# A graph convolution on one core: one-hot rows made for two quads at once, a node number read as float32 out of two bfloat16 columns, and unit additions placed ahead of the equality

## The chip, the cores and the metric

The kernel runs on one core of a Trainium2 chip. The metric is the device time of one execution in microseconds. A core has five engines with queues of their own: TensorE (PE; its weight loads are shown as PEld), VectorE (DVE), ScalarE (ACT), GpSimd (POOL) and SyncE (SP), which here only issues transfers. Engines wait for each other through semaphores.

## The reference

There are 6,250 nodes with 128 features and 200,000 edges. The layer normalises the nodes, multiplies them by `W_in`, fetches a row for each edge, multiplies it by a filter worked out from 20 edge attributes, sums the products at the edges' other ends, and applies two more small layers and a residual:

```python
h = jnp.maximum(_layernorm(x, axis=-1), 0.0)
x = atomic_embedding @ W_in                      # atomic_embedding is h
W_ij = shifted_softplus(f_ij @ W_f1 + b_f1) @ W_f2 + b_f2
W_ij = W_ij * f_ij_cutoff
x_ij = x[idx_j] * W_ij                           # idx_j = dst, sorted
out = jax.ops.segment_sum(x_ij, idx_i, num_segments=N_ATOMS)   # idx_i = src, in random order
return shifted_softplus(out @ W_o1 + b_o1) @ W_o2 + b_o2       # added to x
```

`dst` is sorted, so the rows fetched by neighbouring edges lie close together. `src` is random, so the sum at the end touches all nodes at any time.

## The kernel before, in words

**Quads.** Edges are taken in chunks of 128 and in quads of four chunks (512 edges), 391 quads in all. Two quads make a super-chunk, which SP loads four quads ahead (`load_sc`): edge attributes `ft`, source numbers `sb`, relative row numbers `rb` (one transfer for each quad, into the lower or the upper 64 partitions) and `wn`, windows of 21 consecutive node rows, each in three bfloat16 parts.

**One iteration of the main loop** (from L938) works on several quads at once, in an order written out by hand: every engine gets its instructions in the order of the program text. For quad q: PE makes `z` (L287); ACT makes `e` in three steps (L292, L293, L298); DVE makes the one-hot rows `oh` (L306) that say which window row each edge takes, and `a` (L321); PE multiplies `oh` by `wn` into `xg` (L336) and `a` by `w2` into `W` (L344); ACT scales `xg` into `xc` (L349); DVE multiplies both into messages (L354).

**The plain quads.** 247 quads end in a scatter. DVE compares source numbers into `eq` (L315), PE multiplies `eq` by the messages into `pp` (L366), so that edges of one chunk with the same source share a sum, and ACT copies this into `s` (L374; five buffers). DVE works out `jf` (L388) and ACT the row numbers `ji` (L395). POOL then issues an indirect transfer for each chunk, which adds rows of `s` to one of four accumulators in DRAM (L414), four to a quad. Two scatters into the same accumulator run one after the other.

**The sorted quads.** The other 144 quads, about three in eight, avoid the scatter. Their edges are given one of 16 groups of 392 nodes (`rank_group` and what follows), with 32 slots for each group. DVE makes the permutation `pm` (L499) from `iot`, a row of counting numbers; the messages in `pt` are split in place into three bfloat16 parts (L513), and `ext` puts two more columns behind them (L516): the node's number in its group less 196, and the group. PE permutes all that into `pq` (L523), ACT casts it to `mst` (L531), and DVE adds 196 to the number again to make `lo` (L535). Six sorted quads together make a round, which is summed in four units: DVE makes one-hot columns `so` from `iot` and `lo` (L604), PE multiplies (72 matmuls, L619) into four PSUM buffers, all that the tag B has, and DVE adds these to `accT` in SBUF (L628, L630). What does not fit in the slots is the overflow: two sorted quads share a buffer `mo`, go through an equality of their own (`over_idx`, `over_dg`, `over_row`, `over_eq`, `over_sum`) and end in one scatter.

**Hooks.** Everything beside the plain path is hung on points of an iteration with `at(i, point, ...)`: "D0", "D1", "DM" and "D2" stand between DVE's instructions, "A0" to "A2" between ACT's, "PE2" after PE's, "L" ahead of the iteration, "S" after the scatters. So a hook says in which iteration and behind which instruction its work is queued. On the same hooks, from quad 7 on and every nine quads, hang the 24 further groups of nodes that are normalised and multiplied by `W_in` (`prep_*`), and the splitting of the edge attributes (`fb_*`).

**The tail** (from L1058) loads three of the accumulators, adds them to `accT` and applies the two last layers.

The functions that the change touches:

Of the kernel before, what the change touches and what calls it, by code (L numbers as in the profile page):

```python
# [32 lines left out]
PW = 386  # L33
# [11 lines left out]
def tile_gnn(ctx: ExitStack, tc: tile.TileContext, x, fB, cT, srcT, srcr, dstr, win_, wf1, wf2, bias, bo1c, wo1,  # L45
# [19 lines left out]
    ACC_R = NP + P  # L65
    ZR = 10 if ACC_R % 10 == 0 else 1
# [3 lines left out]
    GN = NP // GRP  # L70
# [50 lines left out]
    iot = cp.tile([P, SLOTS], F16, name="iot")  # L121
# [179 lines left out]
    def s1_oh(q):  # L301
        rb = loads[q // 2][2]
        j = q % 2
        oh = wk.tile([P, 512], BF16, tag="oh", name="oh")
        v = slice(j * HB, (j + 1) * HB)
        nc.vector.tensor_scalar(oh[v], rb[v], rowid[v], None, op0=ALU.is_equal)  # L306
        st[q]["oh"] = oh
# [116 lines left out]
    def rank_group(r):  # L424
        qs = mpq[RKQ * r:RKQ * r + RKQ]
        nc4 = 4 * len(qs)
        srcf = wk.tile([P, 4 * RKQ], F32, tag="srcf", name="srcf", bufs=1)
        for k, q, d, n in runs(qs):
            o = srcf[:, 4 * k:4 * (k + n)]
            nc.vector.tensor_copy(o if n == 1 else o.rearrange("p (j c) -> p j c", c=4), quad_cols(srcT_sb, q, d, n))  # L430
        srcf = srcf[:, :nc4]
        n = [P, nc4, GRP - 1]
        nc.vector.tensor_tensor(ge[:, :nc4, 1:GRP], srcf.unsqueeze(2).to_broadcast(n),
                                thr.unsqueeze(1).to_broadcast(n), op=ALU.is_ge)
        G = wk.tile([P, 4 * RKQ, GRP], BF16, tag="G", name="G", bufs=1)
# [91 lines left out]
    def perm_out(q, s):  # L527
        a, b = divmod(s, 2)
        if b == 0:
            mp[q]["ms", a] = wk.tile([P, 2, PW], BF16, tag=f"ms{a}", name="mst", bufs=RND + 2 + 2 * a)  # L530
        nc.scalar.copy(mp[q]["ms", a][:, b], mp[q].pop(("q", s))[:, :PW])  # L531

    def perm_loc(q, a):
        lo = wk.tile([P, 2], F32, tag=f"lo{a}", name="lo", bufs=RND + 2 + 2 * a)
        nc.vector.tensor_scalar(lo, mp[q]["ms", a][:, :, 3 * P], float(GN // 2), None, op0=ALU.add)  # L535
        mp[q]["lo", a] = lo

    def over_pe(q):
        h = mpi[q] % 2 * OVC
        t = ps.tile([P, 512], F32, tag="B", name="po", bufs=4)  # L540
        o = t[h:h + OVC]
        for c in range(4):
            w = mp[q]["pm"][:, c, GRP * CAP:]
            pt = high(mp[q]["pt"][:, c:c + 1])[:, 0]
            nc.tensor.matmul(o[:, :P + 2], w, pt[:, 2 * P:PW], start=(c == 0), stop=False)
            nc.tensor.matmul(o[:, :P], w, pt[:, P:2 * P], start=False, stop=False)
            nc.tensor.matmul(o[:, :P], w, pt[:, :P], start=False, stop=(c == 3))
        mp[q]["po"] = t

    def over_out(q):  # L550
        h = mpi[q] % 2 * OVC
        mo = mos[mpi[q] // 2 % 2]
        nc.scalar.copy(mo[h:h + OVC, :P + 2], mp[q].pop("po")[h:h + OVC, :P + 2])

    def over_idx(q):
        mo = mos[mpi[q] // 2 % 2]
        so = sp_.tile([P, 1], F32, tag="ovs", name="ovs", bufs=2)
        nc.vector.scalar_tensor_tensor(so, mo[:, P + 1:P + 2], float(GN), mo[:, P:P + 1], op0=ALU.mult, op1=ALU.add)
        mp[q]["so"] = so

    def over_dg(q):
# [3 lines left out]
        jd = sp_.tile([P, 2], F32, tag="ojd", name="ojd", bufs=2)  # L565
# [13 lines left out]
    def over_sum(q):  # L579
        t = ps.tile([P, 512], F32, tag="B", name="osum", bufs=4)  # L580
        nc.tensor.matmul(t[:, :P + 3], mp[q]["eq"], mos[mpi[q] // 2 % 2][:, :P + 3], start=True, stop=True)
        mp[q]["sum"] = t

    def over_copy(q):
        s = sp_.tile([P, 132], F32, tag="os", name="os", bufs=2)
        nc.scalar.copy(s[:, :P + 3], mp[q].pop("sum")[:, :P + 3])
        mp[q]["os"] = s

    def over_ji(q):
        s, jd = mp[q]["os"], mp[q]["jd"]  # L590
        nc.vector.scalar_tensor_tensor(jd[:, 1:2], s[:, P + 2:P + 3], wgt2, jd[:, 0:1], op0=ALU.is_lt, op1=ALU.mult)
# [71 lines left out]
    with tc.manual_schedule():  # L663
# [9 lines left out]
        nc.gpsimd.iota(iot, pattern=[[1, SLOTS]], base=0, channel_multiplier=0, allow_small_or_imprecise_dtypes=True)  # L673
# [86 lines left out]
        for mo_ in mos:  # L760
            nc.vector.tensor_copy(mo_[:, P + 2:P + 3], wgt)
# [142 lines left out]
        for q in mpq:  # L904
# [33 lines left out]
        for i in range(max(NQ + 7, last + 14, r0_end + 2)):  # L938
# [358 lines left out]
```

## Time and profile before

| what | value |
|---|---|
| median of 3 runs | 2198.53 us (2196.79 to 2199.58) |
| the profiled execution: time, span | 2198.7 us, 2196.8 us |
| mean granted TensorE clock | 0.962 |
| PE, weight loads | 1913.6 us (87%), 1373.2 us (63%) |
| DVE | 1886.5 us (86%), 5123 instructions |
| ACT | 1787.2 us (81%) |
| POOL | 1751.8 us (80%) |
| scatters issued by POOL (L414) | 987 of 1621 ns and 72 of 1613 ns |

The span runs from the first to the last instruction; what lies around it is 1.9 us. A group's line in the profile gives: line, engine and operation, what it writes and reads, how often, then its busy time in us and the mean of one in ns, then the idle time of its engine just before it and what ended that. "issue" is time in which an engine waited for nothing that the profile shows. A row of the timeline gives start and duration in us, and in brackets the idle time before. A line of the waits gives the total in us, the number of times and the longest.

### The profile page before, as it was taken

How to read it: one execution, taken by the hardware profiler on the slowest of the kernel's cores; microseconds unless marked ns; L12 is line 12 of the kernel's file. 1: busy time of each engine (PE TensorE's matmuls, PEld its weight loads, DVE VectorE, ACT ScalarE, POOL GpSimd, SP SyncE). 2: the span in 40 equal slices, each digit the busy share in tenths (PEclk: the TensorE clock that was granted, in tenths of full speed). 3: DMA queues.
4: the chain of work that ended last, by engine and by line, in shares of the span. 5: the costliest groups of instructions: out<-in, count | busy, mean ns of one | idle time of the engine just before them, and what ended most of it. 6: DMA issues, size and time to landing. Idle time of an engine off the chain costs nothing.

```text
span 2196.8 us, 55656 instructions
## 1 busy us (share of the span) xinstructions
PE 1913.6 (87%) x19201; PEld 1373.2 (63%) x19201; DVE 1886.5 (86%) x5123; ACT 1787.2 (81%) x4749; POOL 1751.8 (80%) x1101
## 2 busy tenths in 40 slices
PE   3779899898989989988988999999999989899946
PEld 2556666666656666666666667666666666666724
DVE  5688999988888988898989999989889889898935
ACT  4688888888879887878888989888889888888814
POOL 2678888888888887878778888888888888888884
PEclk9799999999999999999999999999999999999977
DMA  8977777776767676767677667677767766767638
GB/s 263 248 168 145 132 143 144 141 143 125 148 128 145 132 145 129 144 122 148 131 138 143 134 136 148 124 142 144 143 121 148 136 140 129 142 127 152 129 37 235
DMA packets 396414, 316.96 MB, mean 144 GB/s; under 512 B 91839, under 2 KB 335722, under 8 KB 396130
## 3 DMA queue, kind: packets, MB, share of 16 engines
q1 hardware_dynamic: 242546, 240.57, 37.2%
q0 software_dynamic: 153296, 72.75, 33.9%
q8 instruction: 151, 2.47, 0.5%
q14 instruction: 133, 1.09, 0.2%
q10 hardware_dynamic: 288, 0.07, 0.0%
HBM read 173.32 MB, written 139.90 MB: 143 GB/s over the span
## 4 chain that ended last, share of the span: by engine, by line
DVE 34%; PE 20%; ACT 18%; DMA 10%; POOL 9%; issue 7%; SPq 2%; ACTq 0%; DVEq 0%; POOLq 0%
POOL acc L414 9%; DMA acc<-s,ji 6%; PE pq L523 4%; ACT xc L349 4%; PE W L344 4%; PE pp L366 4%; DVE pt L513 4%; DVE so L604 3%; DVE pm L499 3%; DVE a L321 3%; DVE eq L315 3%; ACT mst L531 3%; DVE accT L630 3%; PE un L619 3%; ACT e L293 2%
## 5 line engine op out<-in xcount | busy, mean ns | idle before, releaser
L414 POOL DMA_INDIRECT acc<-s,ji x987 | 1599.8, 1621 | 375.7 <-issue 237.3
L523 PE MATMUL pq<-pt,pm 128*128 128x386 bf16 x2304 | 461.6, 340 | 32.8 <-ACT s L374 26.1
L344 PE MATMUL W<-w,a 128*128 128x128 f32 x3128 | 467.0, 294 | 0.0
L349 ACT ACTIVATE xc<-xg,cT_sb 128x128 f32<-128x128 f32 x1564 | 447.1, 374 | 18.0 <-PE xg L336 14.4
L344 PEld LDWEIGHTS W<-w,a 128*128 128x128 f32 x3128 | 391.3, 196 | 42.5 <-issue 3.3
L619 PE MATMUL un<-so,mst 32*128 32x392 bf16 x6912 | 337.6, 330 | 40.7 <-DVE pr L463 9.4
L366 PE MATMUL pp<-m,eq 128*128 128x129 f32 x1976 | 282.9, 287 | 83.2 <-DVE accT L630 61.2
L523 PEld LDWEIGHTS <-pm 128*128 128x128 bf16 x2304 | 225.6, 99 | 190.1 <-issue 46.2
L366 PEld LDWEIGHTS pp<-m,eq 128*128 128x128 f32 x1976 | 263.6, 197 | 125.3 <-DVE accT L630 86.9
L619 PEld LDWEIGHTS <-mst 32*128 32x128 bf16 x6912 | 208.8, 94 | 164.2 <-issue 60.2
L321 DVE SCALAR_TENSOR_TENSOR a<-z,e 128x512 f32<-128x512 f32 x391 | 266.4, 681 | 49.3 <-ACT e L298 47.3
L374 ACT COPY s<-pp 128x258 f32<-128x258 f32 x494 | 175.1, 393 | 147.2 <-PE pp L366 90.7
L298 ACT ACTIVATE e<-e,con 128x512 f32<-128x512 f32 x391 | 282.4, 722 | 12.7
L293 ACT ACTIVATE e<-e 128x512 f32<-128x512 f32 x391 | 246.5, 631 | 12.4
L531 ACT CAST mst<-pq 128x386 bf16<-128x386 f32 x576 | 246.6, 479 | 10.2 <-PE pq L523 10.2
L292 ACT ACTIVATE e<-z 128x512 f32<-128x512 f32 x391 | 238.6, 610 | 16.2 <-PE z L287 15.9
L630 DVE TENSOR_TENSOR accT<-un,accT 128x392 f32<-128x392 f32 x368 | 182.0, 554 | 38.9 <-PE un L619 23.2
L513 DVE TENSOR_TENSOR pt<-pt 128x512 f32<-128x512 f32 x288 | 198.3, 689 | 0.0
L354 DVE TENSOR_TENSOR m<-W,xc 128x512 f32<-128x512 f32 x247 | 168.1, 681 | 33.7 <-ACT xc L349 28.2
L499 DVE TENSOR_SCALAR pm<-iot,pos 128x576 bf16<-128x576 f16 x576 | 190.4, 392 | 0.0
L354 DVE TENSOR_TENSOR pt<-W,xc 128x512 f32<-128x512 f32 x144 | 99.1, 688 | 87.8 <-ACT xc L349 77.3
L315 DVE TENSOR_TENSOR eq<-sb,srcT_sb 128x512 f32<-128x512 int16 x247 | 168.3, 682 | 3.1
(156 smaller groups left out, 2768.4 us busy)
## 6 DMA issues: line engine op xcount, KB each, us to landing
sb<-src SPq DMA_DIRECT2D x195, 256.0 KB
ft<-fsd SPq DMA_DIRECT2D x195, 240.0 KB
rb<-reld SPq DMA_DIRECT2D x391, 64.0 KB
fsd<-f SPq DMA_DIRECT2D x49, 480.0 KB
acc<-s,ji POOLq DMA_INDIRECT x987
fb<-in_fB_dram SPq DMA_DIRECT2D x49, 320.0 KB
fsd<-f SPq DMA_DIRECT2D x49, 320.0 KB
wn<-tab SPq DMA_DIRECT2D x782, 15.8 KB
```

The lines of the kernel that those rows point to most:

```text
L293: nc.scalar.activation(e, e, AF.Exp, scale=-1.0)
L298: nc.scalar.activation(e, e, AF.Ln, bias=half, scale=0.5)
L321: nc.vector.scalar_tensor_tensor(a, st[q]["z"], 0.0, st[q]["l"], op0=ALU.max, op1=ALU.add)
L344: nc.tensor.matmul(W[:, c, :], st[q]["a"][:, c * P:(c + 1) * P], w2, start=False, stop=(c == 3))
L349: nc.scalar.mul(xc[:, c, :], st[q]["xg"][:, c, :], cT_sb[:, 4 * q + c:4 * q + c + 1])
L354: nc.vector.tensor_tensor(m[:, :, :P], st[q]["W"], st[q]["xc"], op=ALU.mult)
L366: nc.tensor.matmul(pp[:, c, :129], st[q]["eq"][:, k, :], m[:, k, :129], start=True, stop=True)
L414: nc.gpsimd.indirect_dma_start(out=accs[k][:, :], out_offset=bass.IndirectOffsetOnAxis(ap=ji, axis=0), in_=s, in_offset=None, compute_op=A ...
L513: nc.vector.tensor_tensor(pt[:, :, k * P:(k + 1) * P], a, high(a), op=ALU.subtract)
L523: nc.tensor.matmul(t[:, :PW], mp[q]["pm"][:, c, s * P:(s + 1) * P], high(mp[q]["pt"][:, c:c + 1, :PW])[:, 0], start=(c == 0), stop=(c == 3))
L531: nc.scalar.copy(mp[q]["ms", a][:, b], mp[q].pop(("q", s))[:, :PW])
L619: nc.tensor.matmul(ts[g][:, :GN], mp[q]["ms", s // 2][v, s % 2, k * P:(k + 1) * P], mp[q]["oh"][v], start=(q == qs[0] and k == 0), stop=(q ...
```

## The change

- `s1_oh` is carried out for even quads only and makes the one-hot rows of both quads of a super-chunk in one instruction on 128 partitions.
- `ext` gets a third column, zero, ahead of the number. A float32 whose lower half is zero and whose upper half is a bfloat16 has the bfloat16's value, so `unit_oh` reads the pair of columns of `mst` as one float32 scalar. The counting row gets 196 more numbers in front (-196 to -1), so that no addition is needed; `perm_loc` and its two hooks go. Rows of `pt` have 387 words for 386, rows of `mst` 388 for 386, and the overflow's columns move by one.
- `over_dg` hangs on "A0" of the next iteration, where it was on "A2", with three buffers for `ovs` and `ojd` where there were two.
- In the main loop the hooks of "D1" (the unit additions) stand ahead of `s1_eq`.

```diff
-PW = 386
+PW = 387
+MW = 388
...
-    iot = cp.tile([P, SLOTS], F16, name="iot")
+    iotw = cp.tile([P, GN // 2 + SLOTS], F16, name="iot")
+    iot = iotw[:, GN // 2:]
...
     def s1_oh(q):
-        rb = loads[q // 2][2]
-        j = q % 2
-        oh = wk.tile([P, 512], BF16, tag="oh", name="oh")
-        v = slice(j * HB, (j + 1) * HB)
-        nc.vector.tensor_scalar(oh[v], rb[v], rowid[v], None, op0=ALU.is_equal)
-        st[q]["oh"] = oh
+        if q % 2 == 0:
+            rb = loads[q // 2][2]
+            oh = wk.tile([P, 512], BF16, tag="oh", name="oh")
+            v = slice(0, min(2, NQ - q) * HB)
+            nc.vector.tensor_scalar(oh[v], rb[v], rowid[v], None, op0=ALU.is_equal)
+            late["oh"] = oh
+        st[q]["oh"] = late["oh"]
...
-        ext = wk.tile([P, 4 * RKQ, 2], BF16, tag="ext", name="ext")
-        nc.vector.tensor_scalar(ext[:, :nc4, 0], loc[:, :nc4], float(-GN // 2), None, op0=ALU.add)
-        nc.vector.tensor_copy(ext[:, :nc4, 1], cnt[:, :nc4])
+        ext = wk.tile([P, 4 * RKQ, 3], BF16, tag="ext", name="ext")
+        nc.vector.memset(ext[:, :, 0], 0.0)
+        nc.vector.tensor_scalar(ext[:, :nc4, 1], loc[:, :nc4], float(-(GN // 2)), None, op0=ALU.add)
+        nc.vector.tensor_copy(ext[:, :nc4, 2], cnt[:, :nc4])
...
-            mp[q]["ms", a] = wk.tile([P, 2, PW], BF16, tag=f"ms{a}", name="mst", bufs=RND + 2 + 2 * a)
-        nc.scalar.copy(mp[q]["ms", a][:, b], mp[q].pop(("q", s))[:, :PW])
-
-    def perm_loc(q, a):
-        lo = wk.tile([P, 2], F32, tag=f"lo{a}", name="lo", bufs=RND + 2 + 2 * a)
-        nc.vector.tensor_scalar(lo, mp[q]["ms", a][:, :, 3 * P], float(GN // 2), None, op0=ALU.add)
-        mp[q]["lo", a] = lo
+            mp[q]["ms", a] = wk.tile([P, 2, MW], BF16, tag=f"ms{a}", name="mst", bufs=RND + 2 + 2 * a)
+        nc.scalar.copy(mp[q]["ms", a][:, b, :PW], mp[q].pop(("q", s))[:, :PW])
...
             so = wk.tile([P, GN], BF16, tag="so", name="so", bufs=RND)
-            nc.vector.tensor_scalar(so, iot[:, :GN], mp[q]["lo", s // 2][:, s % 2:s % 2 + 1], None, op0=ALU.is_equal)
+            w = mp[q]["ms", s // 2].bitcast(F32)
+            nc.vector.tensor_scalar(so, iotw[:, :GN], w[:, s % 2, 3 * P // 2:3 * P // 2 + 1], None, op0=ALU.is_equal)
...
-        nc.gpsimd.iota(iot, pattern=[[1, SLOTS]], base=0, channel_multiplier=0, allow_small_or_imprecise_dtypes=True)
+        nc.gpsimd.iota(iotw, pattern=[[1, GN // 2 + SLOTS]], base=-(GN // 2), channel_multiplier=0, allow_small_or_imprecise_dtypes=True)
...
-            at(q + 4, "DM", perm_loc, q, 0)
-            at(q + 5, "DM", perm_loc, q, 1)
             at(q + 4, "PE2", over_pe, q)
             at(q + 5, "A0", over_out, q)
             if mpi[q] % 2:
                 at(q + 5, "DM", over_idx, q)
-                at(q + 5, "A2", over_dg, q)
+                at(q + 6, "A0", over_dg, q)
...
             if i < NQ:
                 s1_oh(i)
+            run(i, "D1")
             if 0 <= i - 1 < NQ:
                 s1_eq(i - 1)
-            run(i, "D1")
```

More of the change, by code (lines that the diff above doesn't have):

```diff
@@ L65, in tile_gnn @@
     ACC_R = NP + P
+    GN = NP // GRP
     ZR = 10 if ACC_R % 10 == 0 else 1
@@ L69, in tile_gnn @@
     CE = min(128, EP // P)
-    GN = NP // GRP
     mpq = sorted_quads(NQ)
@@ L544, in over_pe @@
             pt = high(mp[q]["pt"][:, c:c + 1])[:, 0]
-            nc.tensor.matmul(o[:, :P + 2], w, pt[:, 2 * P:PW], start=(c == 0), stop=False)
+            nc.tensor.matmul(o[:, :P + 3], w, pt[:, 2 * P:PW], start=(c == 0), stop=False)
             nc.tensor.matmul(o[:, :P], w, pt[:, P:2 * P], start=False, stop=False)
@@ L552, in over_out @@
         mo = mos[mpi[q] // 2 % 2]
-        nc.scalar.copy(mo[h:h + OVC, :P + 2], mp[q].pop("po")[h:h + OVC, :P + 2])
+        nc.scalar.copy(mo[h:h + OVC, :P + 3], mp[q].pop("po")[h:h + OVC, :P + 3])
     def over_idx(q):
         mo = mos[mpi[q] // 2 % 2]
-        so = sp_.tile([P, 1], F32, tag="ovs", name="ovs", bufs=2)
-        nc.vector.scalar_tensor_tensor(so, mo[:, P + 1:P + 2], float(GN), mo[:, P:P + 1], op0=ALU.mult, op1=ALU.add)
+        so = sp_.tile([P, 1], F32, tag="ovs", name="ovs", bufs=3)
+        nc.vector.scalar_tensor_tensor(so, mo[:, P + 2:P + 3], float(GN), mo[:, P + 1:P + 2], op0=ALU.mult, op1=ALU.add)
         mp[q]["so"] = so
@@ L564, in over_dg @@
         mp[q]["dg"] = dg
-        jd = sp_.tile([P, 2], F32, tag="ojd", name="ojd", bufs=2)
+        jd = sp_.tile([P, 2], F32, tag="ojd", name="ojd", bufs=3)
         nc.scalar.activation(jd[:, 0:1], mp[q]["so"], AF.Identity, bias=off)
@@ L580, in over_sum @@
         t = ps.tile([P, 512], F32, tag="B", name="osum", bufs=4)
-        nc.tensor.matmul(t[:, :P + 3], mp[q]["eq"], mos[mpi[q] // 2 % 2][:, :P + 3], start=True, stop=True)
+        nc.tensor.matmul(t[:, :P + 4], mp[q]["eq"], mos[mpi[q] // 2 % 2][:, :P + 4], start=True, stop=True)
         mp[q]["sum"] = t
@@ L585, in over_copy @@
         s = sp_.tile([P, 132], F32, tag="os", name="os", bufs=2)
-        nc.scalar.copy(s[:, :P + 3], mp[q].pop("sum")[:, :P + 3])
+        nc.scalar.copy(s[:, :P + 4], mp[q].pop("sum")[:, :P + 4])
         mp[q]["os"] = s
@@ L590, in over_ji @@
         s, jd = mp[q]["os"], mp[q]["jd"]
-        nc.vector.scalar_tensor_tensor(jd[:, 1:2], s[:, P + 2:P + 3], wgt2, jd[:, 0:1], op0=ALU.is_lt, op1=ALU.mult)
+        nc.vector.scalar_tensor_tensor(jd[:, 1:2], s[:, P + 3:P + 4], wgt2, jd[:, 0:1], op0=ALU.is_lt, op1=ALU.mult)
     def over_int(q):
@@ L760, in tile_gnn @@
         for mo_ in mos:
-            nc.vector.tensor_copy(mo_[:, P + 2:P + 3], wgt)
+            nc.vector.tensor_copy(mo_[:, P + 3:P + 4], wgt)
         if NQ > 2:
```

## The prediction

> **What bounds the kernel now.** I read the page's engine totals first, then the groups of instructions, then GpSimd's timeline and its waits stage by stage. The totals alone mislead:
>
> ```profile
> PE 1913.6 (87%) x19201; PEld 1373.2 (63%) x19201; DVE 1886.5 (86%) x5123; ACT 1787.2 (81%) x4749; POOL 1751.8 (80%) x1101
> DVE 34%; PE 20%; ACT 18%; DMA 10%; POOL 9%; issue 7%; SPq 2%; ACTq 0%; DVEq 0%; POOLq 0%
> ```
>
> Four engines lie between 80 and 87%, and the chain that ended last (second line) gives VectorE (DVE) the most. By these, less work on DVE would be worth much. But the costliest group of all is the scatter that GpSimd (POOL) issues, with a mean of 1.62 us and idle time before it that nothing but "issue" ends:
>
> ```profile
> L414 POOL DMA_INDIRECT acc<-s,ji x987 | 1599.8, 1621 | 375.7 <-issue 237.3 <-ACT ji L395 49.3 <-DMA acc<-s,ji 35.4
> ```
>
> In POOL's timeline (start, duration, idle before) one scatter follows the other with the same 0.30 us between them; only now and then a longer gap, ended by ScalarE's (ACT's) index `ji`, shows that POOL had run dry:
>
> ```profile
> 1601.58 1.54 POOL L414 DMA_INDIRECT acc<-s,ji  x1 [0.30 <-issue]
> 1603.43 1.54 POOL L414 DMA_INDIRECT acc<-s,ji  x1 [0.31 <-ACT mst L531]
> 1605.28 1.54 POOL L414 DMA_INDIRECT acc<-s,ji  x1 [0.30 <-issue]
> ...
> 973.14 1.54 POOL L414 DMA_INDIRECT acc<-s,ji  x1 [0.30 <-issue]
> 978.98 1.60 POOL L414 DMA_INDIRECT acc<-s,ji  x1 [4.29 <-ACT ji L395]
> ```
>
> The 0.30 us is a fixed price of each scatter, not a wait. So POOL's own account is: first scatter at 48.87 us; 1059 scatters of 1.620 = 1716.0; 1058 fixed gaps of 0.305 = 322.7; longer gaps beyond the fixed one 52.6; last scatter ends at 2140.1; the tail to 2196.8 takes 56.7. POOL is full from 49 to 2140 us but for those 52.6 us. Stage by stage they are: up to 350 us 30.6, 350 to 860 us 0.1, 860 to 1215 us 19.5, 1215 to 2020 us 0.1, after that 2.5. The early ones, and the last 2.5, mostly name the landing of an earlier scatter (one to three of the four buffers are in use early, so a scatter waits for an earlier one into the same buffer); there the index had been ready for about 20 us. Only the stage from 860 to 1215 us is short of indices. Waits of POOL in that stage (total, times, longest), and ACT's waits in it and, after the dots, from 1500 to 2020 us:
>
> ```profile
> POOL acc L414 <- issue: 41.2, 135, 0.3
> POOL acc L414 <- ACT ji L395: 23.1, 12, 6.1
> ACT s L374 <- PE pp L366: 22.3, 18, 3.1
> ...
> ACT s L374 <- DMA acc<-s,ji: 21.4, 11, 3.7
> ```
>
> The twelve waits hold 23.1 us, of which 12 fixed gaps are 3.7: 19.5 us are real. Later the pressure is reversed: ACT waits for a buffer `s` (five of them) that POOL has not emptied. I measured the lead as the time from the end of `ji` to the quad's first scatter: about 20 us from 100 to 450 us (the five buffers), falling to 4 by 700 us, 0 to 5 from 760 to 1215 us, and back at 20 by 1500 us, where it stays to the end. The quads are slower than POOL while the 24 node groups are prepared beside them (to about 1170 us), and faster afterwards.
>
> **The change, part by part.** The groups concerned:
>
> ```profile
> L306 DVE TENSOR_SCALAR oh<-rb,con 64x512 bf16<-64x512 bf16 x391 | 141.8, 363 | 8.7 <-DMA rb<-reld 2.4
> L535 DVE TENSOR_SCALAR lo<-mst 128x2 f32<-128x2 bf16 x288 | 72.9, 253 | 15.4 <-ACT mst L531 13.1
> L315 DVE TENSOR_TENSOR eq<-sb,srcT_sb 128x512 f32<-128x512 int16 x247 | 168.3, 682 | 3.1
> L366 PE MATMUL pp<-m,eq 128*128 128x129 f32 x1976 | 282.9, 287 | 83.2 <-DVE accT L630 61.2 <-ACT s L374 10.9 <-DVE accT L628 4.8
> L563 ACT ACTIVATE dg<-idt,ovs 128x128 f32<-128x128 f32 x72 | 29.3, 407 | 52.2 <-DVE ovs L558 52.0
> L513 DVE TENSOR_TENSOR pt<-pt 128x512 f32<-128x512 f32 x288 | 198.3, 689 | 0.0
> ```
>
> *One-hot rows for two quads.* 391 instructions of 64x512 become 196 of 128x512. Duration goes with the columns, so 195 x 0.363 = 70.8 us leave DVE. The pair needs both `rb` transfers of its super-chunk, the second issued some 0.5 us after the first; all were loaded four quads ahead, and the `wn` rows that the same matmuls need are issued after both, so the wait costs nothing (without that lead, at most 0.6 us a pair). Each tile now serves four quads' time instead of two, more room than before.
>
> *The node read as float32.* 288 `lo` leave: 72.9 us, and the 13.1 us that DVE waits there for `mst`. Against it: 18 memsets of 128x32 (nearest: the 128x32 cast into `ext`, 0.234), 4.2 us; four more elements in each of the 144 copies into `pt` (0.189 each), under 1 us. `so` keeps its shape and count, only its scalar comes from `mst`, ready long before. Permutes get one column: 2304 x 0.340/386 = 2 us of PE; with the overflow's extra columns under 1 us more; the evacuations 576 x 0.479/386 = 0.7 us of ACT. The longer iota (0.61 us for 576 columns, 0.82 for 772) adds 0.2 us to POOL at 7 us, hidden by the index load that lands at 13 us.
>
> *Sum for DVE:* 70.8 + 72.9 - 5 = 139 us of 1886, 7%.
>
> *Unit additions ahead of the equality.* 46 of the 96 units have an `eq` that now follows the four additions. It stood 0.60 us ahead of them (start to start), and TensorE (PE), whose four B banks the unit holds, waits 61.2 us for `accT`: up to 46 x 0.6 = 28 us less. Moved behind, `eq` delays `a` of the next quad by nothing, since both were already behind the additions; it is late only where the additions wait for the last unit matmul (23.2 us in all, 11 times), and it is read one iteration later.
>
> *`dg` one iteration later.* ACT no longer waits 52 us for `ovs`. Its two instructions (0.407 + 0.287) now stand ahead of the `mst` casts, `ji` and `xc` of the next iteration; they stood in this queue before. `orow` on PE needs `dg` in the same iteration: around 1010 us ACT's point A0 runs some 2 us ahead of PE's point, so I cost it at 0; if that lead is gone, `orow` and the permutes behind it wait up to the 0.69 us, 72 times, 50 us. SP's queue and the order of the scatters are as before.
>
> *What this does to the end.* On the chain from 350 to 1215 us, `oh` has 21.5 us (half goes: 10.7), `lo` 6.9, and `eq` ahead of additions about 41/96 of 28 = 12: 30 us, without the waits of ACT. The quads lost 19 us of lead and 19.5 of gaps there, 38.5 in all. Relief of 19.5 is enough to close the gaps; 30 leaves 11 us of lead. So the 19.5 us go, and nothing more: the other 110 us saved on DVE become idle time under a full POOL. What is late next is the scatter itself.
>
> *Does a scatter get shorter?* Its median is 1.543 and its mean 1.620, in all 82 us over the median. I sorted the scatters by what DVE ran beside them: 143 with none of the suspects 1.556, 37 with an `oh` alone 1.561, 46 with `lo` alone 1.544, 42 with `pm` alone 1.605, 7 with `eq` alone 1.819. [...] By the trace, `oh` and `lo` cost nothing and `eq`, which stays, costs 0.26. I follow the trace: 1 us, and keep 21 for the low end.
>
> *What speaks against.* `pt` gets rows of 387 words, so rows 1 and 3 begin on an odd word. No row of the trace has that. [...]
>
> *Total:* 2198.7 (profiled execution: span 2196.8 and 1.9 around it) - 19.5 - 1 = 2178.2. The profiled time lies 0.2 us over the median 2198.53, so nothing is corrected. A measurement of this kernel can tell about 0.2%, 4.4 us, from no change.
>
> **The rivals.**
> 1. *DVE is a bound throughout.* Then 139 us times its 34% of the chain, plus PE's 28: about 75 us, 2124. Against it: 0.1 us of gaps in 1315 us of two stages. Chance 0.03.
> 2. [...] Chance 0.08.
> 3. *The relief misses the stage:* `oh` and `lo` go, but the chain moves to PE and ACT, half of the gaps stays: 2188. Chance 0.14.
> 4. *Scatters lengthen.* DVE's two-input work now piles up in bursts beside them. Stage means were 1.604 to 1.637; at 1.637 throughout, 1059 x 0.017 = 18 us come back: 2196, no change. Chance 0.08.
> 5. *Odd rows slow PE.* A permute matmul reads rows of `pt`; if the 1152 that read an odd row took twice the 0.17 us that they are apart, PE would get 196 us more. 83 us of it fall before 1215 us, less 30 of relief: 53 us of new gaps, 2198.7 + 53 = 2252. It decides from a loss of 30 us in that stage, 0.06 us a matmul. For it: PE is 90% busy there. Against it: the reads already step over every second half-word at full rate. Chance 0.05.
>
> The main case has 0.62.
>
> **How the numbers follow.** The main case spans 2170 to 2184 (gaps 0 to 5 us left, stage means of the scatter moving by 0.008 either way). With rival 3 and part of 2, 2163 to 2191 leaves out rival 1, rivals 4 and 5 and some of 2: 0.2. Faster: main 0.62, rivals 1 to 3 0.25, less 0.02: 0.85. Same: most of rival 4 and a little of 3: 0.09. Slower: rival 5 and the far end of 4: 0.06.
>
> **What would show it.** Right: POOL's waits for `ji` from 860 to 1215 us fall from 23.1 to under 5 us; scatters still of 1.62 us with 0.30 between them; the lead stays over 5 us at 1000 us; ACT's waits for the landing of `acc` grow; DVE busy near 1747. `oh` x196 at about 0.36. Wrong: gaps of over 0.4 us still adding to 20 us after 350 us; a scatter mean under 1.60 or over 1.635; `pt` over 0.70 or `pq` slower by 10%. A span under 2160 would refute POOL as the bound.

## The result and the profile after

| | before | after |
|---|---|---|
| median, 4 runs of each on one chip | 2197.66 us (2194.13 to 2199.58) | 2160.73 us (2158.51 to 2169.22) |
| ratio after / before, 95% interval | | 0.9841 (0.9811 to 0.9871) |
| profiled execution: time, span, mean granted clock | 2198.7, 2196.8 us, 0.962 | 2169.22, 2166.6 us, 0.960 |

The changed kernel is 37 us faster; 2178 was forecast, with a range that ended at 2163. The profiled execution of the changed kernel is the slowest of its four, 8.5 us over their median. A second profile of it, taken with the first experiment, has a span of 2156.5 us and stands nearer to the median, so both are used below.

First the page's engine totals of the changed kernel, and under them its chain of waits by engine:

```profile
PE 1910.9 (88%) x19201; PEld 1371.3 (63%) x19201; DVE 1769.9 (82%) x4658; ACT 1781.2 (82%) x4749; POOL 1733.1 (80%) x1101
ACT 23%; PE 20%; DVE 16%; POOL 15%; DMA 15%; issue 9%; SPq 2%; ACTq 0%; DVEq 0%; POOLq 0%
```

DVE's busy time falls by 116.6 us and its part of the chain by more than half. The shares still name no bound. The groups (busy time and mean of one, then the idle time before and its releaser) answer to those shown of before:

```profile
L417 POOL DMA_INDIRECT acc<-s,ji x987 | 1583.2, 1604 | 360.3 <-issue 235.1 <-DMA acc<-s,ji 49.0 <-ACT ji L398 27.4
L308 DVE TENSOR_SCALAR oh<-rb,con 128x512 bf16<-128x512 bf16 x195 | 72.5, 372 | 2.6 <-DMA rb<-reld 2.6
L318 DVE TENSOR_TENSOR eq<-sb,srcT_sb 128x512 f32<-128x512 int16 x247 | 168.3, 681 | 0.0
L369 PE MATMUL pp<-m,eq 128*128 128x129 f32 x1976 | 273.7, 282 | 39.1 <-DVE accT L630 22.6 <-ACT s L377 6.1 <-ACT mst L535 3.9
L562 ACT ACTIVATE dg<-idt,ovs 128x128 f32<-128x128 f32 x72 | 28.2, 392 | 2.9 <-DVE ovs L557 2.9
L517 DVE TENSOR_TENSOR pt<-pt 128x512 f32<-128x512 f32 x288 | 198.7, 690 | 0.0
L527 PE MATMUL pq<-pt,pm 128*128 128x387 bf16 x2304 | 464.6, 341 | 52.5 <-ACT s L377 47.2 <-ACT h L198 2.7 <-DVE pt L517 1.7
```

The first line is the surprise: the mean scatter went from 1621 to 1604 ns, although nothing about a scatter was changed. Next POOL's waits from 860 to 1215 us, the three largest (total, times, longest), and ACT's largest wait for a landing in the whole span:

```profile
POOL acc L417 <- issue: 45.6, 149, 0.5
POOL acc L417 <- ACT mst L535: 2.7, 9, 0.3
POOL acc L417 <- DMA acc<-s,ji: 2.7, 9, 0.3
...
ACT s L377 <- DMA acc<-s,ji: 71.2, 39, 6.0
```

No wait of that stage is longer than 0.5 us: the index is always there, and it is ACT that now waits for POOL to empty `s`. POOL's account, with all 1059 scatters in it, each 0.305 us behind the last (322.7 us in every column):

| us | before | after | after, second profile |
|---|---|---|---|
| first scatter starts | 48.9 | 49.3 | 49.2 |
| 1059 scatters, total (mean) | 1716.0 (1.620) | 1696.9 (1.602) | 1692.5 (1.598) |
| gaps beyond 0.305, total | 52.6 | 39.7 | 34.9 |
| of these from 860 to 1215 us | 19.5 | 0.2 | 0.0 |
| last scatter to end of span | 56.7 | 58.0 | 57.2 |

The spans of the first two columns differ by 30.2 us: 19.1 from shorter scatters, 12.9 from gaps, less 1.7 in start and tail. The gaps lost 19.3 in the stage that was short of indices and got 6.4 back elsewhere, all at waits for landings. So the gaps of that stage went as forecast, 19.3 of 19.5 us; the shorter scatters were not forecast.

### The profile page after: what moved, and what is told of

Same layout as the page of the kernel before. It is cut to its first block, busy times and chain, and to the rows that moved or that the text cites. A ratio compares the mean times of both kernels' runs of the same rounds, so it can differ in the third digit from the quotient of the medians.

```text
span 2166.6 us, 55320 instructions
## 1 busy us (share of the span) xinstructions
PE 1910.9 (88%) x19201; PEld 1371.3 (63%) x19201; DVE 1769.9 (82%) x4658; ACT 1781.2 (82%) x4749; POOL 1733.1 (80%) x1101
## 4 chain that ended last, share of the span: by engine, by line
ACT 23%; PE 20%; DVE 16%; POOL 15%; DMA 15%; issue 9%; SPq 2%; ACTq 0%; DVEq 0%; POOLq 0%
POOL acc L417 15%; DMA acc<-s,ji 12%; ACT xc L352 5%; PE un L619 5%; PE W L347 5%; ACT e L295 3%; ACT mst L535 3%; PE pq L527 3%; ACT e L294 3%; PE pp L369 3%; ACT e L300 3%; ACT s L377 2%; DVE pm L503 2%; DVE so L604 2%; DVE a L324 1%
## 5 line engine op out<-in xcount | busy, mean ns | idle before, releaser
L417 POOL DMA_INDIRECT acc<-s,ji x987 | 1583.2, 1604 | 360.3 <-issue 235.1
L527 PE MATMUL pq<-pt,pm 128*128 128x387 bf16 x2304 | 464.6, 341 | 52.5 <-ACT s L377 47.2
L352 ACT ACTIVATE xc<-xg,cT_sb 128x128 f32<-128x128 f32 x1564 | 445.8, 373 | 25.1 <-PE xg L339 22.6
L619 PE MATMUL un<-so,mst 32*128 32x392 bf16 x6912 | 342.8, 333 | 40.3 <-DVE rm L217 11.1
L619 PEld LDWEIGHTS <-mst 32*128 32x128 bf16 x6912 | 201.4, 95 | 177.9 <-issue 62.0
L369 PE MATMUL pp<-m,eq 128*128 128x129 f32 x1976 | 273.7, 282 | 39.1 <-DVE accT L630 22.6
L295 ACT ACTIVATE e<-e 128x512 f32<-128x512 f32 x391 | 246.5, 630 | 12.4
L535 ACT CAST mst<-pq 128x387 bf16<-128x387 f32 x576 | 246.9, 481 | 11.6 <-PE pq L527 11.6
L289 PE MATMUL z<-ft,ws 123*128 123x512 bf16 x391 | 152.9, 392 | 19.5 <-DMA ft<-fsd 10.3
```

The source lines that it names most:

```text
L295: nc.scalar.activation(e, e, AF.Exp, scale=-1.0)
L352: nc.scalar.mul(xc[:, c, :], st[q]["xg"][:, c, :], cT_sb[:, 4 * q + c:4 * q + c + 1])
L369: nc.tensor.matmul(pp[:, c, :129], st[q]["eq"][:, k, :], m[:, k, :129], start=True, stop=True)
L417: nc.gpsimd.indirect_dma_start(out=accs[k][:, :], out_offset=bass.IndirectOffsetOnAxis(ap=ji, axis=0), in_=s, in_offset=None, compute_op=A ...
L527: nc.tensor.matmul(t[:, :PW], mp[q]["pm"][:, c, s * P:(s + 1) * P], high(mp[q]["pt"][:, c:c + 1, :PW])[:, 0], start=(c == 0), stop=(c == 3))
L535: nc.scalar.copy(mp[q]["ms", a][:, b, :PW], mp[q].pop(("q", s))[:, :PW])
```

## The experiments

Two theories stood after that. *Theory A, the lock:* a `tensor_scalar` on VectorE holds scatters up for as long as it runs, as the 1.605 us of the 42 scatters beside `pm` alone may say (1.556 beside none of the suspects); so taking away 288 `lo` and 195 `oh` shortens scatters. That was my assumption. *Theory B, the beginning:* something about how the equality comes to stand beside the start of a scatter. Each experiment was run beside the kernel before on the same chip; ratios are to that.

**The changed kernel again,** for a second profile and as the base of what follows.

> The changed kernel once more, as the base of the runs beside it. Its first profile closed the gaps of GpSimd between 860 and 1215 us (19.5 to 0.2 us, as forecast) and had scatters of 1.602 us where the kernel before had 1.620, which was not forecast; its median was 2160.7 us, its profiled run 2169.2. If the shorter scatter belongs to the change, the mean is again near 1.60 and the time 2157 to 2166 us. If it was the spread between executions, the mean comes out anywhere from 1.60 to 1.62 and the time up to 2178 us.

Measured: 2159.81 us against 2198.53, ratio 0.983 (0.9816 to 0.9845).

**One part taken back at a time.** From the changed kernel: the one-hot rows made for each quad again, as the removed lines of the diff have it; `lo` made again (288 instructions, read by `so`); the equality ahead of the additions again, with `over_dg` on "A2" of its old iteration.

```diff
# lo made again
+        nc.vector.tensor_scalar(lo, mp[q]["ms", a][:, :, 3 * P + 1], float(GN // 2), None, op0=ALU.add)
...
# equality first again
-                at(q + 6, "A0", over_dg, q)
+                at(q + 5, "A2", over_dg, q)
...
-            run(i, "D1")
             if 0 <= i - 1 < NQ:
                 s1_eq(i - 1)
+            run(i, "D1")
```

> The changed kernel with one-hot rows made for each quad again (391 instructions of 64x512). [...] Rival (these instructions cost a scatter nothing, as the sorting in the prediction had it; the gain was lead alone): under 3 us, since the lead of 5 to 10 us at 1100 us shrinks but does not run out.

> The changed kernel with the 288 small additions that make the node number back in their old places, and the one-hot columns reading their result. [...] Rival: under 3 us, as GpSimd stays full.

> The changed kernel with the equality ahead of the unit additions again and the overflow's diagonal back one iteration earlier on ScalarE. No work is added on VectorE, so the lock theory gives scatters of the same length and, as the lead covers the later additions, 0 to 3 us. Rival (the order is what shortened the scatters, by parting the one-hot instruction from the two-input equality behind it): the scatter mean rises by 0.005 to 0.015, the time by 5 to 15 us.

| taken back | median us | ratio (interval) | scatters, total | gaps 860 to 1215 |
|---|---|---|---|---|
| nothing | 2159.8 | 0.983 (0.9816 to 0.9845) | 1692.5 | 0.0 |
| the merged one-hot | 2177.0 | 0.9898 (0.988 to 0.9916) | 1705.0 | 6.1 |
| no `lo` | 2167.7 | 0.986 (0.9844 to 0.9876) | 1696.6 | 0.0 |
| the order, `dg` | 2166.5 | 0.9857 (0.9839 to 0.9874) | 1694.7 | 9.3 |

The one-hot rows are the part that shortens scatters (12.5 us, where two profiles of the changed kernel differ by 4.4). The order acts through gaps alone: the mean scatter rose by 0.002 us, as the first reading of that run had it, but not with its 0 to 3 us. Its line of POOL's waits from 860 to 1215 us is the old one in small:

```profile
POOL acc L417 <- ACT ji L398: 12.3, 10, 5.0
```

`lo` cost 8 us, where the rival had under 3. Its trace has 4.1 us more of scatters and 4.0 more of gaps than the second profile of the changed kernel, but the first profile has as much of both; so where the 8 us lie is not shown.

**The one-hot rows alone.** The kernel before with only the new `s1_oh`.

> The kernel before with one-hot rows for two quads at once and nothing else of the change. Lock theory and lead together: scatters shorter by 0.012 us (12 us), and of the 19.5 us of gaps some 7 to 10 gone: 2176 to 2181 us. Rival (the part works only together with the others): over 2185 us.

Measured: 2168.37 us against 2198.93, ratio 0.9867 (0.9846 to 0.9889). The scatters come to 1689.1 us, as short as in the whole change, while 11.8 us of gaps stay in the middle stage. This part alone brings 31 of the 39 us, and is 8 us faster than the range expected of it. Its group of scatters:

```profile
L415 POOL DMA_INDIRECT acc<-s,ji x987 | 1575.5, 1596 | 369.5 <-issue 234.8 <-DMA acc<-s,ji 48.9 <-ACT ji L396 45.0
```

**The lock, tested by putting work back.** To the changed kernel, one more DVE instruction for every odd quad, so that it stands where the second `oh` was: a memset (no `tensor_scalar`, so without a lock by Theory A), a one-hot of 128 rows whose result is not used, or an equality of 192 columns that isn't used either.

```diff
         st[q]["oh"] = late["oh"]
+        if q % 2:                                    # memset
+            pad = wk.tile([P, 272], F32, tag="pad", name="pad")
+            nc.vector.memset(pad, 0.0)
...
+            # or: 128 rows, one input
+            nc.vector.tensor_scalar(pad, loads[q // 2][2], rowid, None, op0=ALU.is_equal)
...
+            # or: two inputs, 192 columns
+            nc.vector.tensor_tensor(pad, loads[q // 2][1][:, :192].rearrange("p (c i) -> p c i", c=2),
+                                    srcT_sb[:, q * 4:q * 4 + 2].unsqueeze(2).to_broadcast([P, 2, 96]), op=ALU.is_equal)
```

> The changed kernel with one instruction more on VectorE in each odd quad, where the second one-hot instruction stood: a memset of 128x272 float32 into a tile that nobody reads, about 0.35 us, 68 us in all. [...]Lock theory: the scatter mean stays at 1.598 to 1.602; only the lead shrinks, and the gaps from 860 to 1215 us come back by about 7 us as in the kernel with split one-hot rows; the time is 2162 to 2170 us. Rival (any work on VectorE at this place lengthens scatters, by moving the two-input instructions behind it): the mean rises to 1.610 and the time to about 2177 us.

> The same with a one-hot instruction (tensor_scalar, 128x512 bfloat16 from SBUF to SBUF, about 0.35 us) into a tile that nobody reads. Lock theory: as with split one-hot rows, a scatter mean of about 1.610 and 2174 to 2180 us, so 8 to 12 us more than with the memset of the same length at the same place. Rival: the same as with the memset.

> The same with a small equality of two SBUF inputs (tensor_tensor, 128x192, about 0.36 us) into a tile that nobody reads. In the sorting of the kernel before, scatters beside the large equality were the longest (1.82 us). [...]

By source line in each kernel's trace (shortest/mean/longest in ns, then where in the span) the one-hot and the two-input pad cost DVE the same, the memset a little less:

```profile
L313 DVE MEMSET pad<- x195: 285/285/285, 28.0 to 2051.4; 128x272 f32 x195
L313 DVE TENSOR_SCALAR pad<-rb,con x195: 334/349/634, 28.1 to 2052.8; 128x512 bf16<-128x512 bf16 x195
L313 DVE TENSOR_TENSOR pad<-sb,srcT_sb x195: 337/351/391, 27.9 to 2054.1; 128x192 f32<-128x192 int16 x195
```

All three are by ratio about 9 us slower than the changed kernel: 2169.21, 2170.12 and 2170.40 us, ratios 0.9868, 0.987 and 0.987. The scatters' means were 1.605, 1.596 and 1.603, the gaps of the middle stage 0.3, 8.5 and 3.8 us. Theory A expected the longest scatters beside the one-hot, at 1.610; they are shortest there. Of the memset it expected 1.598 to 1.602 and some 7 us of gaps; that was missed too. An extra 68 us of one-hots leaves the scatters at 1690.2 us in all, 2.3 under the second profile, so their lengthening does not follow the busy time of such instructions; what this run lost is gaps.

The lock itself is there all the same, when single scatters are looked at. A pad, and a scatter that starts in it, of the kernel with the 128-row pad:

```profile
395.08 0.35 DVE L313 TENSOR_SCALAR pad<-rb,con 128x512 bf16<-128x512 bf16 x1
395.20 1.64 POOL L420 DMA_INDIRECT acc<-s,ji  x1 [0.30 <-issue]
```

The pad has 0.23 us left when the scatter starts, and the scatter is 0.10 us longer than the median of 1.543. The table takes all scatters that start 0.06 us or more into an instruction with 0.15 us or more of it left, and compares what they have over the median with what is left of the instruction, less 0.126 us:

| kernel | instruction, its length in us | large inputs | scatters | longer by just that (within 0.005 us) | less than 0.01 us longer | lost, us |
|---|---|---|---|---|---|---|
| before | `so`, 0.31 | one, SBUF | 42 | 42 | 0 | 3.8 |
| before | `pm`, 0.36 | one, SBUF | 47 | 43 | 2 | 3.1 |
| after, 128-row pad | pad, 0.35 | one, SBUF | 24 | 13 | 8 | 2.8 |
| before | `eq`, 0.68 | two, SBUF | 37 | 34 | 0 | 12.3 |
| before | `pt` (L513), 0.69 | two, SBUF | 79 | 69 | 0 | 22.6 |
| before | `a`, messages, `accT`, 0.56 to 0.68 | two, one of them in PSUM | 226 | 0 | 210 | 0.5 |

(Two of the 24 in the pad are held by the equality behind it as well.) So `so` and `pm`, with one input, hold a scatter by the same law (85 of 89) as `eq` and `pt` with two (103 of 116). What Theory A had wrong is the size: a scatter that starts in the first 0.06 us of a `so` or `pm`, or in its last 0.126 us, loses next to nothing by it (under 0.01 us in 97 of 117 such cases in the kernel before). An estimate from these figures, with a scatter every 1.97 us that starts anywhere: an instruction of 0.35 us costs 0.164² / 2 / 1.97 = 0.007 us on average, so 195 pads 1.3 us (the 2.8 of the table have 1.5 from the two that the equality held), too little for the mean to show; one of 0.69 us costs 0.064 us, nine times as much.

**The equality without a second input.** In the changed kernel, each equality as four instructions that compare with a scalar.

```diff
-        nc.vector.tensor_tensor(eq, sb[:, j * SEG:(j + 1) * SEG].rearrange("p (c i) -> p c i", c=4),
-                                srcT_sb[:, q * 4:q * 4 + 4].unsqueeze(2).to_broadcast([P, 4, P]), op=ALU.is_equal)
+        for c in range(4):
+            k = 4 * (q % 8) + c
+            nc.vector.tensor_scalar(eq[:, c], sb[:, j * SEG + c * P:j * SEG + (c + 1) * P], late["sf"][:, k:k + 1],
+                                    None, op0=ALU.is_equal)
```

> The changed kernel with each equality of the plain quads (one tensor_tensor of two SBUF inputs, 0.68 us) replaced by four tensor_scalar of 128x128 with the source number as a float32 scalar, and one conversion of 32 source columns for eight quads. Theory formed from the runs so far: a scatter whose start falls into an instruction with two SBUF inputs waits for that instruction's end; scatters that start in an equality hold 12 to 16 us of excess in the changed kernel. They vanish, the scatter mean falls from about 1.600 to about 1.587, and the time to 2143 to 2155 us, though VectorE gets more work. [...]

Measured: 2169.11 us against 2195.11, ratio 0.9877 (0.9862 to 0.9892); the expected time was missed. The scatters did shorten, to 1682.6 us, and what scatters lost at an equality fell from 12.4 to 2.1 us. But 988 of about 0.28 us are 277 us of DVE where there were 168, and 16.3 us of gaps came back in the middle stage. Both halves of the account at work: scatters shorter, indices later. It is not the second input alone that went: of 47 scatters that start 0.06 us or more into one of the short pieces with 0.15 us or more left, 31 are longer by the same law; a piece of 0.28 us only has little left to hold with.

**One-hot rows on 128 partitions, but still for every quad.** The kernel before, with all 391 `oh` made over the full height. The order of DVE's instructions is that of before, and a one-hot takes 0.368 us for 0.363; only the height differs.

```diff
-        v = slice(j * HB, (j + 1) * HB)
+        v = slice(0, min(2, NQ - (q - j)) * HB)
```

> The kernel before, with each of its 391 one-hot instructions on all 128 partitions where it had 64 (half of the rows are made and not read). VectorE's work stays the same, so the gaps of 19.5 us stay. In the kernel before, scatters that start in a 64-row one-hot instruction with an equality right behind it waited through both (29 scatters, 16 us); behind a 128-row one they slipped in between. If the width is the reason: the mean falls from 1.620 to about 1.605, the time to 2178 to 2188 us. If the number of instructions is: no change, 2194 to 2203 us.

Measured: 2177.22 us against 2195.11, ratio 0.9917 (0.9904 to 0.9929). Scatters 1702.0 us, 14 less than before, and the middle gaps 11.1, which were expected to stay at 19.5. Writing twice as many rows, half of them for nothing, makes the kernel 18 us faster.

**The same pad on 64 and on 128 partitions.** The 128-row pad above, cut to half its rows.

```diff
-            nc.vector.tensor_scalar(pad, loads[q // 2][2], rowid, None, op0=ALU.is_equal)
+            nc.vector.tensor_scalar(pad[:HB], loads[q // 2][2][:HB], rowid[:HB], None, op0=ALU.is_equal)
```

> The changed kernel with an extra one-hot instruction in each odd quad into a tile that nobody reads, as in the run with 128 rows (2170 us, scatter mean 1.596), but on 64 partitions. VectorE's time is the same. If the width is what makes a scatter that starts in it wait through the equality behind it too: the scatter mean rises to 1.603 to 1.612 and the time by 5 to 12 us over the one with 128 rows, to 2175 to 2182 us. If the width does not matter: 2167 to 2173 us.

Measured: 2181.03 us against 2195.19, ratio 0.9934 (0.9911 to 0.9957), where the full height gave 0.987 (0.9851 to 0.9888). The scatter groups with the pad of 128 rows and of 64, and the second pad's line:

```profile
L420 POOL DMA_INDIRECT acc<-s,ji x987 | 1575.3, 1596 | 371.6 <-issue 230.6 <-DMA acc<-s,ji 44.5 <-ACT ji L401 44.0
```

```profile
L420 POOL DMA_INDIRECT acc<-s,ji x987 | 1598.6, 1620 | 356.6 <-issue 238.0 <-DMA acc<-s,ji 35.1 <-ACT ji L401 33.5
L313 DVE TENSOR_SCALAR pad<-rb,con x195: 329/340/659, 28.0 to 2063.8; 64x512 bf16<-64x512 bf16 x195
```

The same place, 9 ns less of duration, half the rows: 1620 for 1596 ns, 22.7 us over 1059 scatters. That is more than the part that was not forecast; but only about 9 of the 22.7 us are scatters held just ahead of an equality (the table below), the rest lies mostly at `pm` and `pt`.

**What happens at the start of a scatter.** The timelines (start, duration) show it one by one. The kernel before, even quad; before, odd quad; the changed kernel's second profile; the 64-row pad:

```profile
317.35 0.33 DVE L306 TENSOR_SCALAR oh<-rb,con 64x512 bf16<-64x512 bf16 x1
317.61 0.67 DVE L315 TENSOR_TENSOR eq<-sb,srcT_sb 128x512 f32<-128x512 int16 x1
317.58 2.12 POOL L414 DMA_INDIRECT acc<-s,ji  x1 [0.30 <-issue]
...
445.25 0.35 DVE L306 TENSOR_SCALAR oh<-rb,con 64x512 bf16<-64x512 bf16 x1
445.63 0.69 DVE L315 TENSOR_TENSOR eq<-sb,srcT_sb 128x512 f32<-128x512 int16 x1
445.54 1.54 POOL L414 DMA_INDIRECT acc<-s,ji  x1 [0.30 <-issue]
```

```profile
1223.24 0.34 DVE L308 TENSOR_SCALAR oh<-rb,con 128x512 bf16<-128x512 bf16 x1
1223.50 0.69 DVE L318 TENSOR_TENSOR eq<-sb,srcT_sb 128x512 f32<-128x512 int16 x1
1223.47 1.54 POOL L417 DMA_INDIRECT acc<-os,oji  x1 [0.30 <-issue]
```

```profile
1209.08 0.34 DVE L313 TENSOR_SCALAR pad<-rb,con 64x512 bf16<-64x512 bf16 x1
1209.34 0.68 DVE L321 TENSOR_TENSOR eq<-sb,srcT_sb 128x512 f32<-128x512 int16 x1
1209.30 2.14 POOL L420 DMA_INDIRECT acc<-s,ji  x1 [0.30 <-issue]
```

All four scatters start while a one-hot runs and an equality is about to follow. Behind these 128 rows, or behind the odd quad's 64 (where the equality begins only after `oh` has ended), the scatter takes its 1.54 us. Behind the even quad's 64 rows, or the 64-row pad, it is held by the equality: its end, 317.61 + 0.67 = 318.28, less 317.58, leaves 0.70; the scatter is 0.58 longer than the median of 1.543.

Two counts over whole traces show how general that is. First, 698 scatters in the traces of this case start 0.06 us or more inside an equality with 0.15 us or more of it left: 663 are longer than the median by (end of equality − start of scatter) − 0.126 us to within 0.005. Those that start in `a`, the messages or `accT` lose next to nothing (0.5 us in all for 226 in the kernel before), and so do those in `lo` (0.02 us for 11). Second, the scatters that start from 0.19 us before an equality to 0.02 after its start, "held" when over 0.2 us longer than the median:

| kernel | what runs ahead of the equality | scatters | held | lost, us |
|---|---|---|---|---|
| before | `oh`, 64 rows, even quads | 23 | 23 | 14.5 |
| before | `oh`, 64 rows, odd quads | 13 | 0 | 0.1 |
| before, `oh` on 128 rows | `oh`, 128 rows | 16 | 3 | 2.2 |
| one-hot rows alone | `oh`, 128 rows, or other | 21 | 0 | 0.6 |
| after, and its second profile | `oh`, 128 rows, or other | 19, 27 | 0, 0 | 0.4, 0.5 |
| after, the merged one-hot taken back | `oh`, even quads, or `accT` | 16 | 16 | 9.8 |
| after, 128-row pad | pad, `oh` or `accT` | 24 | 3 | 2.6 |
| after, 64-row pad | pad | 11 | 11 | 7.1 |
| after, 64-row pad | `oh` on 128 rows, or `accT` | 20 | 7 | 4.2 |
| after, memset pad | memset | 12 | 12 | 6.6 |
| after, memset pad | `oh` or `accT` | 12 | 0 | 0.0 |
| before, half the plain scatters | `oh`, 64 rows, even quads | 28 | 28 | 17.1 |
| after, half the plain scatters | `oh`, 128 rows | 17 | 12 | 8.7 |

So 14.2 of the 19.1 us by which scatters shortened are the ones that were held just ahead of an equality before, and are not now. The rest is spread over the other instructions that hold scatters and moves from run to run with where scatters fall. In 10 of the 23 held ones of before, `oh` had more than 0.126 us left: by the law above `oh` held them first, and the equality took over.

Why they are not held now is open in part. The last row shows the same `oh` of the changed kernel holding 12 scatters; one of them, at 1199.83 us:

```profile
1199.75 0.34 DVE L308 TENSOR_SCALAR oh<-rb,con 128x512 bf16<-128x512 bf16 x1
1200.01 0.68 DVE L318 TENSOR_TENSOR eq<-sb,srcT_sb 128x512 f32<-128x512 int16 x1
1199.83 2.28 POOL L417 DMA_INDIRECT acc<-s,ji  x1 [1.28 <-ACT ji L398]
```

Over all traces, of scatters that start within 0.055 us of the equality's start or up to 0.02 us after it, 8 of 111 are held behind 128 rows (`oh` or one-hot pad) and 31 of 31 behind 64 rows that overlap the equality; of those that start 0.055 to 0.19 us ahead, 17 of 29 and 37 of 37. In the two profiles of the changed kernel all 17 behind `oh` fall into the near stretch; before, 10 of the 23 (6.9 of the 14.5 us) fell into the far one. So a part of the gain comes from the height, and a part from where scatters happened to fall; no run parts the two.

Nor is it the row count of the instruction just ahead alone: with a 64-row pad in the quad, some scatters behind a 128-row `oh` are held too. What goes with it is how far VectorE's instructions overlap. In the 13 traces with all scatters and the one-piece equality, where the equality began 72 to 76 ns before the end of the instruction ahead of it, 47 of 55 scatters in that window were held; at 77 or 78 ns, 14 of 50; at 79 or more, 15 of 167 (12 of these behind the memset); where it began after that end, none of 22. In the kernel before, even quads overlap by 72 to 78 ns, in the changed kernel all mostly by 76 to 88. At half load it fails: of 20 scatters at 79 ns or more 10 were held. It is a correlation; what sets the overlap wasn't tried by itself.

**Is POOL still the bound?** Every second scatter of the plain quads left out, in the kernel before and in the changed one; the sums of plain edges lack that half.

```diff
-        for c in range(nchunks(q)):
+        for c in range(0, nchunks(q), 2):
```

> The kernel before with the scatters of chunks 1 and 3 of each plain quad left out (565 left, so the sums lack half of the plain edges). POOL then has about half its work and no longer bounds: the time is what the other engines need. From the stage with no lead (355 us for 65 quads) and the later rise of the lead: 216 quads of 5.45 us, 171 of 4.85, start and tail 105: about 2110 us (2080 to 2130). If DVE or PE bound all along as the chain has it, 2170 or more.

> The changed kernel with the same scatters left out (sums lack half of the plain edges). Theory: the change takes 139 us off VectorE and some waits off TensorE and ScalarE, of which 30 us of 885 were on the chain between 350 and 1215 us; over the whole loop about 70 us: 2025 to 2060 us, so that the saving that GpSimd hides in the full kernel shows here. If VectorE was not on the path of the quads at all, within 15 us of the kernel before with the same scatters left out.

Measured: 2123.07 us (ratio 0.9671, 0.9657 to 0.9685), as expected, and 2067.38 (0.9419, 0.9405 to 0.9432), 7 us over the range expected. (The stage from 350 to 1215 us is 865 us long, not the 885 of the second expectation.) With POOL at half its load the change saves 55.7 us. The engine totals of the two:

```profile
PE 1895.8 (89%) x19201; PEld 1379.0 (65%) x19201; DVE 1846.8 (87%) x5123; ACT 1778.5 (84%) x4749; POOL 998.2 (47%) x608
```

```profile
PE 1885.0 (91%) x19201; PEld 1373.8 (67%) x19201; DVE 1742.5 (84%) x4658; ACT 1782.7 (86%) x4749; POOL 983.5 (48%) x608
```

With half of the plain scatters the changed kernel needs 2067 us; with all of them GpSimd holds it at 2160. Before, the distance was 2195 − 2123 = 72 us, now 93.

**A further step that the account suggests.** Of the gaps that are left, 32 us lie before 350 us, where few accumulators are in use and a scatter waits for the last one into the same buffer to land. The changed kernel with the fourth accumulator taken into use from 72 on, for 140:

```diff
-    K1_END, K2_END, K3_END = 2, 8, 140
+    K1_END, K2_END, K3_END = 2, 8, 72
```

> The changed kernel with the fourth accumulator in use from scatter 72 on, where it was 140. GpSimd's gaps before 350 us, 31 to 33 us, name the landing of an earlier scatter into the same buffer; between scatters 72 and 140 they hold some 10 us. If that is their cause, they fall by 5 to 10 us, and as GpSimd bounds, so does the time, to 2150 to 2156 us. Rival (the landing is late because of the zeroing and other transfers, whatever the buffer): under 2 us.

Measured: 2153.66 us against 2195.19, ratio 0.9805 (0.9783 to 0.9828). POOL's waits for landings from 100 to 350 us, of the changed kernel and of this one:

```profile
POOL acc L417 <- DMA acc<-s,ji: 12.6, 13, 2.7
```

```profile
POOL acc L417 <- DMA acc<-s,ji: 9.4, 9, 2.6
```

Between scatters 72 and 140 the gaps beyond 0.305 us go from 4.8 and 5.8 us (the two profiles of the changed kernel) to 0.0; these had been put at 10. By ratios the gain over the changed kernel is 5.5 us (0.983 to 0.9805); the two intervals overlap, so the time alone does not settle it, the gaps support it. It has the lowest median of the kernels with all scatters.

## Why the prediction was wrong, point by point

- **The bound** was right: POOL is full, its account closes after as before, and the half-load runs show 93 us under it. My own criterion for refuting that, "a span under 2160", was badly set: the second profile has 2156.5 with POOL as full as ever. It took the length of a scatter as fixed.
- **The gaps from 860 to 1215 us** were right: 19.5 forecast, 19.3 gone. The shortest lead in that stage is 5.3 us, the median 10.5; the waits for `ji` fell from 23.1 to 0.6 us, the fixed price of two.
- **What failed is the step "Does a scatter get shorter?"** I took 1 us where 19.1 (first profile) to 23.5 (second) were measured, and that term carries the miss: 2178 less 18 is the median. (That the sum closes so well is in part luck: the 6.4 us of longer waits in the last point below were not in it either, and the profiled execution lies 8.5 us over the median.) The sorting behind it looked at scatters beside an `oh` *alone* (1.561) and set aside those beside `oh` *and* `eq`. The cost sits in just these: in the kernel before, 29 scatters start at any point of an even quad's `oh` with `eq` next and lose 0.549 us each, 15.9 us (the window of the table of held ones has 23 of them). The rows for `eq` alone (1.819, only 7) should have been the warning that the equality holds scatters, and that what stands ahead of it bears on how many. Nor does an `oh` cost nothing, as I read it: by itself it cost 0.8 us, and in 10 cases it handed the scatter on to the equality.
- **The 21 us kept for the low end, and rival 2,** came near the 19.1 us in size, but no run shows that term: it shared out the 82 us by busy time. In its place the runs showed that a lock is there (42 of 42 scatters in `so` are held, 3.8 us in all) and does not go by busy time: an additional 68 us of 128-row `tensor_scalar` left scatters at 1.596 us, and `lo` cost its 11 scatters 0.02 us. A two-input equality lengthens the scatter that starts in it, by all that is left of it but 0.126 us (34 of 37 in the kernel before). In the run with all 391 one-hots made taller no `oh` and no `lo` went, and 14 us were won all the same.
- **`eq` behind the additions** was somewhat better than said: PE's wait for `accT` fell from 61.2 to 22.6 us, 38.6 for 28 at most. **`dg`** waits 2.9 us for `ovs` in place of 52, and `orow` did not pay for it, as costed.
- **The odd rows** of `pt` cost nothing: 0.690 us for 0.689, and `pq` 341 ns for 340. Rivals 4 and 5 fell with that and with the scatters' mean.
- **DVE** lost 116.6 us of busy time, not 139, although `oh` and `lo` lost 69 and 73 as summed. Their durations overlapped the next instruction's: `oh` of 0.33 us is followed after 0.26. A sum of durations overstates what removing short instructions frees. It didn't matter for the end, as said: the rest is idle time.
- **Not foreseen:** 6.4 us of longer waits for landings, found in the first profile. They differ between two profiles of one kernel by nearly 5 us, and no run here settles what sets them.

## What to carry to other kernels

When one engine is full, make its account to the last microsecond, and treat the duration of its own instruction as a thing that others can change, not as a constant. What such another instruction costs does not go with its busy time: here one of 0.69 us cost about nine times one of 0.35, by the estimate above. When instructions overlap, do not sort by "alone": sort by what runs at the moment where the dependent one starts, and by what is queued next. A saving elsewhere is worth only the gaps that it closes (here 12.9 us of gaps, with 116.6 us less of VectorE); a run with half the load on the full engine tells how much of it lies hidden (the changed kernel was 93 us faster so, the one before 72).

## What the runs showed of the hardware that was not expected

- A scatter that POOL issues 0.06 us or more after the start of a VectorE instruction takes longer by what is left of that instruction, less 0.126 us, when that is an `eq` or a `pt` with two SBUF inputs (`eq`: 663 of 698 scatters to within 0.005 us; `pt`: 69 of 79 in the kernel before) and also when it is a `so` or a `pm` with one (85 of 89 there). In the instructions with one input in PSUM (`a`, the messages, `accT`) 210 of 226 lose under 0.01 us.
- Whether a scatter that starts up to 0.19 us ahead of an equality slips in depends on what VectorE ran before and on how far ahead it starts: none of 46 held in the changed kernel's two profiles (17 of them behind `oh`), but 12 of 17 behind the same `oh` at half load, 11 of 11 behind a 64-row pad, and 12 of 12 behind a memset of 128 rows. What decides is not known.
- A one-hot instruction on 64 partitions and one on 128 take nearly the same time (340 and 349 ns), and the taller one made the kernel faster: 18 us with 391 of them, with nothing else changed.
